# Sorted one-hot gathers in a graph transformer: twenty ranges of sixteen slots instead of twenty-two, with a pair's one-hots laid out by node block

## The chip, the cores and the metric

The kernel runs on one core of a Trainium2 chip. The metric is the device time of one execution in microseconds (us). TensorE does the matrix products, VectorE and ScalarE the elementwise work, GpSimd issues the indirect DMAs (gathers), and SyncE issues most of the other transfers. In the profile they are PE (PEld is its weight load), DVE, ACT, POOL and SP.

## The reference

Three layers of a graph transformer over 6250 nodes with 64 features and 206250 edges, sorted by destination:

```python
q, k, v, e = x @ Wq + bq, x @ Wk + bk, x @ Wv + bv, edge_attr @ We
alpha = sum(q[dst] * (k[src] + e), -1) / 8
p = exp(alpha - segment_max(alpha, dst)[dst])
w = p / segment_sum(p, dst)[dst]
x = relu(segment_sum((v[src] + e) * w, dst) + x @ Ws + bs)   # then a layer norm, in the first two layers
```

A log-softmax, a residual with the input and a last layer norm follow. What matters here is `x[src]`: for every edge, the 64 features of its source node.

## The kernel before

**Tiling.** Edges come in 403 chunks of 512 (four tiles of 128 rows). Four chunks make a unit; there are 100 whole units and a short rest in each layer. Nodes lie in 49 blocks of 128. Attention for a unit is: product with the queries (`scores`, L1648), maximum (L1655), exponential (L1662), transposed weights (`weights`, L1674, copied by L1677), weighted sums (`sums`, L1687, copied out by L1695).

**Two ways to fetch a source row.** One is a gather: an indirect DMA on POOL for 128 rows (`take`, L594). The other needs no DMA. The edges of a chunk are sorted once, in the first layer, so that the first `SLOTS = WINDOWS * SL` = 22 * 16 = 352 of its 512 places are *ranges*: range w holds 16 edges whose source lies in the four node blocks 2w to 2w+3. For such a range the rows come from a product of a one-hot matrix (which of the 128 nodes of a block does this edge want?) with the block's features, which lie in SBUF. Neighbouring ranges 2q and 2q+1 make a *pair*: range 2q takes blocks 4q to 4q+3, range 2q+1 takes blocks 4q+2 to 4q+5, so blocks 4q+2 and 4q+3 are in both.

**A job** is one pair for 16 chunks (`TURN` = 4 units), in class `Picker`. `load` (L1289) brings the pair's 512 keys (16 chunks, two ranges, 16 edges; place within the range's four blocks) to all partitions in one transfer of 128 rows of 1 KB. `aim` makes the one-hots: four DVE instructions of 128x512 (L1313), one for each of the four blocks of a range, both ranges at once. `bank` multiplies: for each of the two ranges, four products of 256 columns that add up in PSUM (L1352), 8 in all, and one ACT copy into `kept` (L1360). A pair's results serve four units, so with 11 pairs in layers 1 and 2 the units of a round of four have 3, 3, 3 and 2 jobs. In layer 0, `PAIRS[0]` = 6 pairs are used: 192 of a chunk's places, and only from unit 8 on.

**From `kept` to the unit.** `naturals` transposes and adds the two halves of the rows (L1387 in layers 1 and 2, L1376 in layer 0) and DVE copies them into the unit's `feat` (L1392, L1394). In layers 1 and 2 places 0 to 351 come that way: tiles 0 and 1 whole, and `PART` = 96 rows of tile 2. The other `REST` = 32 rows of tile 2, of four chunks, share one gather into the tile `few`, from which four ACT copies of 32 rows (`settle`, L611) take them to their places. Tile 3 is gathered for each chunk. So a unit has five gathers there. A gather waits for a copy of its indices into a `gate` by ACT (L631): that is how its place in time is set (`drip`, `free` and `release`; two units ahead of the unit that uses it).

**The first layer** also sorts: `ranking` seats the edges in ranges, one step for each of `WINDOWS + 1` = 23 kinds (L927, L931, L934, L938, L939), four rankings in all. `Move` reorders a unit's edges by products with 0/1 matrices of `REACH[t]` columns (L1052, L1063, L1077): for tile t of the unsorted edges, the sorted places up to which they can go. `Move.index` (L1108) derives the remaining source indices and writes the keys to DRAM (`keyS`, L1138) in pieces of 64 bytes. If the edges of some chunk do not fit the ranges and reaches, a flag is raised and a second, general program computes everything again after this one.

**Order.** The order is written out by hand. In the loop of layers 1 and 2 PE's order for a unit is: scores, naturals of the next unit, one `bank`, transposes of this unit's rows (L1635), weights, the remaining jobs that are due, sums. DVE's is: maximum, two copies of naturals, one-hots, copy of the weights, further one-hots. Two jobs' one-hots are ready ahead there, in two sets of four tiles; one in layer 0.

Of the kernel before, what the change touches and what calls it, by code (L numbers as in the profile page):

```python
# [36 lines left out]
WINDOWS = 22  # L37
# [14 lines left out]
REACH = (392, 416, 456, CH)  # L52
# [383 lines left out]
def main_path(  # L436
# [91 lines left out]
    def ps(tag):  # L528
        return psum.tile([P, 512], F32, tag=tag, name=f"ps_{tag}", bufs={"a": 2, "x": 2}.get(tag, 1))
# [3 lines left out]
    assert 2 * (WINDOWS - 1) + BW < NB <= 2 * BINS and NT % TURN == 0 and U0 % TURN == 0 and REST * LB == P  # L533
# [12 lines left out]
    keyS = dram.tile([KEYED, NT // TURN + 1, TURN, LB, 2 * SL], FP16, name="keyS")  # L546
# [9 lines left out]
    def fetch(layer, k):  # L556
# [15 lines left out]
        if layer and placed(layer, k):  # L572
            spares[layer, k] = later.tile([P, D], F32, name="few", bufs=FB + 1)

    def rows_wanted(layer, k):
# [6 lines left out]
        return [(None, 0)] + [(c, T - 1) for c in range(m)]  # L582

    def indices(layer, k, c, t):
# [3 lines left out]
        if c is None:  # L588
            return src_b, k * LB * T + (2 * LB - 1 if layer else LB + 1 + t // 2)
        return src_b, k * LB * T + t * LB + c  # L590

    def take(layer, k, c, t, index):

        nc.gpsimd.indirect_dma_start(  # L594
            out=loaded[layer, k][:, c, t, 0] if c is not None else spares[layer, k] if layer else loaded[0, k][:, t, 1, 0],
# [11 lines left out]
    def settle(layer, k):  # L607

        if layer and placed(layer, k):
            for c in range(LB):  # L610
                nc.scalar.copy(  # L611
                    loaded[layer, k][PART:, c, 2, 0], spares[layer, k][c * REST : (c + 1) * REST, :]
                )
# [257 lines left out]
    }  # L871
    stamps = [const.tile([P, LB * T, W], BF16, name=f"stamp{i}") for i in range(2)]
# [137 lines left out]
    class Move:  # L1010
# [97 lines left out]
        def index(self):  # L1108
# [3 lines left out]
            pi = pa[:, : 3 + 2 * LB]  # L1112
            pk = pa[:LB, W : W + KEYED * 2 * SL]
            nc.tensor.matmul(pk, keyc, self.to[:, : KEYED * 2 * SL], start=True, stop=True)
            for t in range(2, T):
                at = 3 + (t - 2) * LB
# [6 lines left out]
            for c in range(LB):  # L1123
                nc.tensor.matmul(
                    pi[c * REST : (c + 1) * REST, 2:3], self.to[:, SLOTS : 3 * P], pickc[:, c : c + 1], start=True, stop=True
                )
            nc.vector.tensor_scalar(
                src_b[:, k * LB * T + LB + 1 : (k + 1) * LB * T], pi, float(N - 1), None, ALU.min
# [133 lines left out]
    class Picker:  # L1262
# [14 lines left out]
        def load(self):  # L1277

            while self.loads and len(self.keys) < (7 if self.layer else 3):
# [3 lines left out]
                shape = [P, TURN * LB * 2 * SL]  # L1283
                if self.layer:
                    key = later.tile(shape, FP16, name="key", bufs=7)
                else:
                    key = picks.tile(shape, FP16, name="key", bufs=3)
                a, b = self.span(job)
# [749 lines left out]
```

## Time and profile before

| | |
|---|---|
| median of 3 runs | 4548.02 us (4546.31 to 4551.62) |
| profiled execution: time, span | 4547.86 us, 4546.1 us |
| busy share of the span: PE, PEld, DVE, ACT, POOL | 82%, 58%, 68%, 54%, 56% |
| mean granted TensorE clock | 0.895 |
| layer 0, steady part 300 to 2100 us: busy PE, DVE, ACT, POOL | 1503, 1216, 882, 1088 us of 1800 |
| layer 1, steady part 2420 to 3220 us: the same | 701, 602, 501, 469 us of 800 |
| layer 2, steady part 3560 to 4400 us: the same | 717, 634, 549, 480 us of 840 |

The span runs from the first to the last instruction of the profiled execution; 1.8 us of its time lie outside. Busy time of an engine is the union of its instructions. A matmul's duration includes the time in which its result still travels through the array, so consecutive ones overlap: what one costs PE is the distance between the starts of neighbours, which the timeline gives (a merged row of n instructions, and the start of the next row). A wait that is ascribed to an engine may have ended with another event at the same time. "remote" is an event whose origin the profile does not show.

### The profile page before, as it was taken

How to read it: one execution, taken by the hardware profiler on the slowest of the kernel's cores; microseconds unless marked ns; L12 is line 12 of the kernel's file. 1: busy time of each engine (PE TensorE's matmuls, PEld its weight loads, DVE VectorE, ACT ScalarE, POOL GpSimd, SP SyncE). 2: the span in 40 equal slices, each digit the busy share in tenths (PEclk: the TensorE clock that was granted, in tenths of full speed). 3: DMA queues.
4: the chain of work that ended last, by engine and by line, in shares of the span. 5: the costliest groups of instructions: out<-in, count | busy, mean ns of one | idle time of the engine just before them, and what ended most of it. 6: DMA issues, size and time to landing. Idle time of an engine off the chain costs nothing.

```text
span 4546.1 us, 106920 instructions
## 1 busy us (share of the span) xinstructions
PE 3750.4 (82%) x35698; PEld 2635.5 (58%) x35698; DVE 3110.5 (68%) x8905; ACT 2434.5 (54%) x6979; POOL 2547.7 (56%) x2094
## 2 busy tenths in 40 slices
PE   5778888888888888888789888888878888888885
PEld 2445555555555555555477666666747666666664
DVE  5566676776766766666477777777746777777784
ACT  2334544544545444544456666666645666666674
POOL 5545566666665665655265655565526655565653
PEclk9788998988989899998789999999878988899997
DMA  5446666667666677776467767777646776777774
GB/s 114 113 125 174 172 177 182 169 177 184 173 172 184 166 188 192 189 185 178 136 154 183 191 168 191 187 178 183 172 112 142 182 175 170 181 182 184 176 186 97
DMA packets 827547, 766.85 MB, mean 169 GB/s; under 512 B 395281, under 2 KB 624935, under 8 KB 826990
## 3 DMA queue, kind: packets, MB, share of 16 engines
q1 hardware_dynamic: 666370, 565.02, 49.8%
q0 software_dynamic: 66688, 68.42, 8.2%
q10 hardware_dynamic: 93932, 126.48, 7.9%
q8 instruction: 288, 4.72, 0.4%
q14 instruction: 269, 2.20, 0.2%
HBM read 599.30 MB, written 160.27 MB: 167 GB/s over the span
## 4 chain that ended last, share of the span: by engine, by line


## 5 line engine op out<-in xcount | busy, mean ns | idle before, releaser
L594 POOL DMA_INDIRECT feat<-in_x,gate x1044 | 1278.7, 1225 | 896.3 <-ACT gate L631 622.0
L1313 DVE TENSOR_SCALAR hot<-key,rank 128x512 fp32r<-128x512 f16 (+2 forms) x2832 | 1165.5, 474 | 144.4 <-DMA key<-keyS 34.6
L594 POOL DMA_INDIRECT feat<-x,gate x816 | 946.3, 1160 | 533.7 <-ACT gate L631 225.3
L1638 ACT COPY featT<-ps_a 64x512 f32<-64x512 f32 x1176 | 682.8, 581 | 86.3 <-remote 21.8
L1352 PE MATMUL ps_x<-hot,halves 128*128 128x256 f32 (+2 forms) x4368 | 684.1, 306 | 19.9 <-ACT kept L1360 9.0
L1352 PEld LDWEIGHTS ps_x<-hot,halves 128*128 128x128 f32 x4368 | 598.0, 202 | 31.8 <-ACT kept L1360 19.1
L1063 PE MATMUL ps_x<-hit,rest 128*64 128x512 bf16 (+3 forms) x3200 | 501.1, 391 | 11.0 <-issue 10.7
L1687 PE MATMUL ps_g<-feat,probT 128*32 128x128 f32 x9672 | 403.2, 295 | 117.7 <-issue 53.0
L594 POOL DMA_INDIRECT few<-x,gate x198 | 283.8, 1433 | 366.1 <-ACT gate L631 138.5
L1655 DVE TENSOR_REDUCE most<-ps_s 128x1 f32<-128x512 f32 x297 | 204.1, 687 | 391.3 <-PE ps_s L1648 156.6
L1052 DVE TENSOR_SCALAR hit<-ruler,pos 128x512 bf16<-128x512 f16 (+3 forms) x1600 | 421.6, 334 | 13.3 <-PE ps_m L1077 12.4
L1360 ACT CAST kept<-ps_x 128x512 fp32r<-128x512 f32 (+2 forms) x546 | 307.3, 582 | 218.1 <-PE ps_x L1352 137.0
L1648 PE MATMUL ps_s<-featT,q 128*32 128x512 f32 x2376 | 405.6, 640 | 11.2 <-issue 7.2
L1687 PEld LDWEIGHTS ps_g<-feat,probT 128*32 128x32 f32 x9672 | 287.1, 117 | 197.4 <-issue 104.5
L1635 PE MATMUL ps_a<-ident,feat 128*128 128x128 f32 x2348 | 353.1, 288 | 41.8 <-ACT gate L631 11.1
L1063 PE MATMUL ps_x<-hit,raw 128*64 128x512 bf16 (+3 forms) x1600 | 332.9, 404 | 8.0 <-issue 7.8
L631 ACT COPY gate<-src_b 128x1 int32<-128x1 int32 x1946 | 325.8, 191 | 20.7 <-ACT eN L1103 15.6
L1635 PEld LDWEIGHTS ps_a<-ident,feat 128*128 128x128 f32 x2348 | 288.6, 149 | 63.8 <-issue 23.2
L1387 PEld LDWEIGHTS ps_m<-twice,kept 128*128 128x128 f32 x1600 | 213.2, 206 | 186.9 <-issue 186.6
L1662 ACT ACTIVATE prob<-ps_s,part 128x512 f32<-128x512 f32 x297 | 204.3, 688 | 185.2 <-issue 33.2
L1063 PEld LDWEIGHTS <-rest 128*64 128x64 bf16 x3200 | 206.5, 123 | 162.3 <-issue 80.1
L1695 ACT COPY part<-ps_g 128x128 f32<-128x128 f32 (+1 forms) x309 | 82.6, 267 | 394.1 <-remote 124.9
(253 smaller groups left out, 5587.3 us busy)
## 6 DMA issues: line engine op xcount, KB each, us to landing
feat<-eaP SPq DMA_DIRECT2D x292, 512.0 KB
featT<-eaS SPq DMA_DIRECT2D x292, 512.0 KB
key<-keyS SPq DMA_DIRECT2D x668, 128.0 KB
raw<-in_ea SPq DMA_DIRECT2D x200, 256.0 KB
eaS<-eT ACTq DMA_DIRECT2D x200, 256.0 KB
eaP<-eN ACTq DMA_DIRECT2D x200, 256.0 KB
to<-toS SPq DMA_DIRECT2D x292, 128.0 KB
part<-part SPq DMA_DIRECT2D x600, 32.5 KB
```

Of the source, the lines that this page charges most:

```text
L594: nc.gpsimd.indirect_dma_start(out=loaded[layer, k][:, c, t, 0] if c is not None else spares[layer, k] if layer else loaded[0, k][:, t, 1, 0],
L631: copy(gate, index[:, i : i + 1])
L1052: nc.vector.tensor_scalar(hit, ruler[:, : REACH[t]], self.pos[:, at : at + 1], None, ALU.is_equal)
L1063: nc.tensor.matmul(self.px[i][j * D : (j + 1) * D, : REACH[t]], self.part(i, part)[:, (j * T + t) * D : (j * T + t + 1) * D], self.hits[t, ...
L1313: nc.vector.tensor_scalar(hot[:, a:b].rearrange("p k w e -> p (k w e)"), self.keys[job][:, a * 2 * SL : b * 2 * SL], rank[:, h : h + 1], None,
L1352: nc.tensor.matmul(px[:, w, a:b], halves[block >= EARLY][:, block - EARLY * (block >= EARLY)].rearrange("p h d -> p (h d)"), made[h][:, a: ...
L1360: nc.scalar.copy(kept[t][:, a:b, at : at + 2 * SL].rearrange("p k (w e) -> p w k e", w=2), px[:, :, a:b])
L1387: nc.tensor.matmul(pn[:, t - ts[0], c], kept[t][:, k % TURN * LB + c], twice, start=True, stop=True)
L1635: nc.tensor.transpose(pt[:, j - js[0], t // 2], rows[:, t * D : (t + 2) * D], ident)
L1638: nc.scalar.copy(featT[:, :, :, h, :], pt[h * D : (h + 1) * D])
L1648: nc.tensor.matmul(self.p_s[rows], self.q[:, j * STRIDE : j * STRIDE + W], self.featT[:, j, :], start=False, stop=True)
L1687: nc.tensor.matmul(p_g[rows, :].rearrange("n (h d) -> n h d", h=2), self.probT[:, t, rows], batch[:, c + j, t], start=(t == 0), stop=(t == ...
```

## The change

There are 20 ranges instead of 22 (`SLOTS` = 320), and the reaches go with it (376, 408, 464, 512 for 392, 416, 456, 512). Layers 1 and 2 use 10 pairs instead of 11, so a round of four units has 3, 3, 2 and 2 jobs. `PART` and `REST` are 64 and 64: the rest of tile 2 takes two gathers for a unit instead of one, and two ACT copies of 64 rows by 128 columns instead of four of 32 by 64.

The one-hots of a pair lie in one tile of eight pieces of 256 columns: block 4q, block 4q+1, block 4q+2 for both ranges, block 4q+3 for both ranges, block 4q+4, block 4q+5. Each of the four DVE instructions now writes two pieces that are not neighbours. A block that is in both ranges is multiplied once, with 512 columns; the four others with 256: 6 products for 8. The keys lie range by range, so a load brings two rows of 512 bytes to each partition, and the keys are written in pieces of 32 bytes. The two sets of one-hots are fixed tiles that are written again and again.

```diff
-WINDOWS = 22
+WINDOWS = 20
-REACH = (392, 416, 456, CH)
+REACH = (376, 408, 464, CH)
...
-        return [(None, 0)] + [(c, T - 1) for c in range(m)]
+        return [(None, c) for c in range(0, m, 2)] + [(c, T - 1) for c in range(m)]
...
-            for c in range(LB):
-                nc.scalar.copy(
-                    loaded[layer, k][PART:, c, 2, 0], spares[layer, k][c * REST : (c + 1) * REST, :]
-                )
+            for i in range(2):
+                nc.scalar.copy(loaded[layer, k][PART:, i::2, 2, 0], spares[layer, k][i * REST : (i + 1) * REST])
...
-                    nc.scalar.dma_start(keyS[those, job, r].rearrange("q c e -> c q e"), key[:, those])
+                    nc.scalar.dma_start(
+                        keyS[those, :, job, r].rearrange("q w c e -> c (q w) e"),
+                        key[:, those].rearrange("c q (w e) -> c (q w) e", w=2),
+                    )
...
-            made = []
-            for h in range(BW):
-                hot = pool.tile([P, TURN * LB, 2, SL], F32R, name="hot", bufs=BW)
+            made = hots[self.aimed % len(hots)]
+            for h, at in enumerate((slice(0, 4, 3), slice(1, 6, 4), slice(2, 7, 4), slice(4, 8, 3))):
                 nc.vector.tensor_scalar(
-                    hot[:, a:b].rearrange("p k w e -> p (k w e)"),
-                    self.keys[job][:, a * 2 * SL : b * 2 * SL],
+                    made[:, at, a * SL : b * SL],
+                    self.keys[job][:, :, a * SL : b * SL],
                     rank[:, h : h + 1],
                     None,
                     ALU.is_equal,
                 )
...
-            for w in range(2):
-                for h in range(BW):
-                    block = 2 * (2 * q + w) + h
-                    assert halved[block] == self.layer
-                    nc.tensor.matmul(
-                        px[:, w, a:b],
-                        halves[block >= EARLY][:, block - EARLY * (block >= EARLY)].rearrange("p h d -> p (h d)"),
-                        made[h][:, a:b, w],
-                        start=(h == 0),
-                        stop=(h == BW - 1),
-                    )
+            x = slice(a * SL, b * SL)
+            there = [px[:, :, x]] * 2 + [px[:, 0, x]] * 2 + [px[:, 1, x]] * 2
+            these = [made[:, 2:4, x], made[:, 4:6, x], made[:, 0, x], made[:, 1, x], made[:, 6, x], made[:, 7, x]]
+            for i, h in enumerate((2, 3, 0, 1, 4, 5)):
+                block = 4 * q + h
+                nc.tensor.matmul(
+                    there[i],
+                    halves[block >= EARLY][:, block - EARLY * (block >= EARLY)].rearrange("p h d -> p (h d)"),
+                    these[i],
+                    start=(i == 0),
+                    stop=(i == 5),
+                )
```

Two places in the order of the instructions, each before and then after. The first is PE in the steady part of layer 1, from the naturals of one unit to the sums; `ps_x` is a job's result, `prob` the weights.

```order
L1387 MATMUL ps_m<-twice,kept_32446 128x64 x4
L1387 MATMUL ps_g<-twice,kept_32447 96x64 x4
L1352 MATMUL ps_x<-hot,halves 128x256 x8
L1635 MATMUL ps_a<-ident,feat 128x128 x8
L1674 MATMUL ps_p<-ident,prob 128x128 x4
L1352 MATMUL ps_x<-hot,halves 128x256 x8
L1352 MATMUL ps_x<-hot,halves_32445 128x256 x8
L1687 MATMUL ps_g<-feat,probT 32x128 x16
```

```order
L1388 MATMUL ps_m<-twice,kept_31500 128x64 x4
L1388 MATMUL ps_g<-twice,kept_31501 64x64 x4
L1352 MATMUL ps_x<-hot,halves 128x512 x2
L1352 MATMUL ps_x<-hot,halves 128x256 x4
L1636 MATMUL ps_a<-ident,feat 128x128 x8
L1675 MATMUL ps_p<-ident,prob 128x128 x4
L1352 MATMUL ps_x<-hots_31499,halves 128x512 x2
L1352 MATMUL ps_x<-hots_31499,halves 128x256 x4
L1352 MATMUL ps_x<-hot,halves_31498 128x512 x2
L1352 MATMUL ps_x<-hot,halves_31498 128x256 x4
L1688 MATMUL ps_g<-feat,probT 32x128 x16
```

Nothing has changed its place: each job is six products instead of eight, and the naturals of tile 2 have 64 rows. The second place is ACT in layer 1, from one unit's `settle` to the next; `gate` releases a gather, `few` holds the rests of tile 2.

```order
L611 COPY feat<-few 32x64 x4
L1662 ACTIVATE prob,part<-ps_s,part 128x512
L631 COPY gate<-src_b 128x1
L1360 CAST kept_254<-ps_x 128x2x16x16
L1638 COPY featT<-ps_a 64x4x128
L631 COPY gate<-src_b 128x1
L1638 COPY featT<-ps_a 64x4x128 x2
L631 COPY gate<-src_b 128x1
L1638 COPY featT<-ps_a 64x4x128
L1360 CAST kept_32446<-ps_x 128x2x16x16
L1360 CAST kept_32447<-ps_x 128x2x16x16
```

```order
L611 COPY feat<-few 64x2x64 x2
L1663 ACTIVATE prob,part<-ps_s,part 128x512
L629 COPY gate<-src_b 128x1 x2
L1360 CAST kept_254<-ps_x 128x2x16x16
L1639 COPY featT<-ps_a 64x4x128 x2
L629 COPY gate<-src_b 128x1
L1639 COPY featT<-ps_a 64x4x128 x2
L629 COPY gate<-src_b 128x1
L1360 CAST kept_31500<-ps_x 128x2x16x16
L1360 CAST kept_31501<-ps_x 128x2x16x16
```

Both gathers of `few` are released together, right behind the exponential; the gathers of tile 3 follow at later points than before in the transposes' copies.

More of the change, by code (lines that the diff above doesn't have):

```diff
@@ L572, in fetch @@
         if layer and placed(layer, k):
-            spares[layer, k] = later.tile([P, D], F32, name="few", bufs=FB + 1)
+            spares[layer, k] = later.tile([P, LB // 2, D], F32, name="few", bufs=FB + 1)
     def rows_wanted(layer, k):
@@ L588, in indices @@
         if c is None:
-            return src_b, k * LB * T + (2 * LB - 1 if layer else LB + 1 + t // 2)
+            return src_b, k * LB * T + LB + t // 2 + (LB // 2 if layer else 0)
         return src_b, k * LB * T + t * LB + c
@@ L871, in main_path @@
     }
+    hots = [picks.tile([P, 2 * BW, TURN * LB * SL], F32R, name="hot", bufs=1)]
     stamps = [const.tile([P, LB * T, W], BF16, name=f"stamp{i}") for i in range(2)]
@@ L1111, in index @@
             pa = ps("a")
[L1112 removed]
+            pi = pa[:, : 3 * LB]
             pk = pa[:LB, W : W + KEYED * 2 * SL]
@@ L1319, in aim @@
                 )
-                made.append(hot)
             self.hots[job] = made
```

33 lines of the change are left out of this document (17 added, 16 removed).

## The prediction

> **What bounds the kernel now.** I read the busy shares first, then the busy times by stage, since half of the change touches layers 1 and 2 only.
>
> ```profile
> PE 3750.4 (82%) x35698; PEld 2635.5 (58%) x35698; DVE 3110.5 (68%) x8905; ACT 2434.5 (54%) x6979; POOL 2547.7 (56%) x2094
> ...
> 300.00:2100.00 1800.00, 1503.10 (x14672) 928.65 (x14668) 1215.60 (x3857) 881.61 (x2529) 1087.90 (x873) 0.90 0.67 178
> ...
> 2420.00:3220.00 800.00, 701.47 (x6978) 547.92 (x6968) 601.81 (x1502) 500.71 (x1458) 469.34 (x375) 0.94 0.73 182
> ```
>
> The columns of the last two rows are the stretch, its length, and PE, PEld, DVE, ACT and POOL busy, then granted clock, DMA share and GB/s. PE is busy 83% of layer 0 and 88% of layer 1, DVE 68% and 75%. No engine is full, but in layer 1 two come near it together. Next the groups of instructions between 2400 and 3200 us, to count work by unit.
>
> ```profile
> L594 POOL DMA_INDIRECT feat<-x,gate x299 | 355.6, 1189 | 187.5 <-ACT gate L631 81.6 <-issue 54.3 <-ACT feat L611 46.4
> L1313 DVE TENSOR_SCALAR hot<-key,rank 128x512 fp32r<-128x512 f16 x818 | 343.4, 484 | 28.2 <-PE ps_x L1352 13.8 <-remote 6.9 <-PE ps_p L1674 3.9
> L1352 PE MATMUL ps_x<-hot,halves 128*128 128x256 f32 x1640 | 254.6, 303 | 11.2 <-ACT kept L1360 5.3 <-DVE hot L1313 4.8 <-issue 1.0
> ...
> L594 POOL DMA_INDIRECT few<-x,gate x75 | 114.4, 1526 | 141.4 <-ACT gate L631 50.3 <-DVE feat L1394 32.2 <-PE ps_x L1352 22.9
> ...
> L1674 PE MATMUL ps_p<-ident,prob 128*128 128x128 f32 x296 | 46.7, 281 | 17.2 <-ACT prob L1662 13.8 <-issue 3.3
> ```
>
> L1674 runs four times a unit, so 74 units took 800 us: 10.8 us each. 1640 products are 205 jobs, 2.77 a unit. What a job costs PE is in the timeline of two undisturbed units (start, length):
>
> ```profile
> 2718.64 0.60 PE L1674 MATMUL ps_p<-ident,prob 128*128 128x128 f32 x4
> 2719.00 2.20 PE L1352 MATMUL ps_x<-hot,halves 128*128 128x256 f32 x16
> 2721.13 1.08 PE L1687 MATMUL ps_g<-feat,probT 128*32 128x128 f32 x32
> ...
> 2723.91 1.08 PE L1387 MATMUL ps_m<-twice,kept 128*128 128x64 f32 x8
> 2724.82 0.51 PE L1387 MATMUL ps_g<-twice,kept 128*96 128x64 f32 x4
> 2725.16 1.22 PE L1352 MATMUL ps_x<-hot,halves 128*128 128x256 f32 x8
> 2726.22 1.04 PE L1635 MATMUL ps_a<-ident,feat 128*128 128x128 f32 x8
> 2727.09 0.60 PE L1674 MATMUL ps_p<-ident,prob 128*128 128x128 f32 x4
> 2727.45 1.23 PE L1352 MATMUL ps_x<-hot,halves 128*128 128x256 f32 x8
> 2728.77 1.08 PE L1687 MATMUL ps_g<-feat,probT 128*32 128x128 f32 x32
> ...
> 2730.84 0.40 PE L1646 MATMUL ps_s<-to,codeT 128*32 128x512 bf16 x4
> ```
>
> No row shows a wait: from weights to weights PE ran through, 8.45 us. Eight products take 1.06 us from start to next start (2725.16 to 2726.22), 0.133 each. DVE in the same unit:
>
> ```profile
> 2726.45 1.67 DVE L1313 TENSOR_SCALAR hot<-key,rank 128x512 fp32r<-128x512 f16 x4
> 2728.04 0.68 DVE L1677 COPY probT<-ps_p 128x512 f32<-128x512 f32 x1
> 2728.64 1.66 DVE L1313 TENSOR_SCALAR hot<-key,rank 128x512 fp32r<-128x512 f16 x4
> ```
>
> A job's one-hots take 1.6 to 1.67 us of DVE, more than its products take of PE, and the sums at 2728.77 start when the copy of the weights ends (28.04 + 0.68). So in layers 1 and 2 the unit is paced by PE and DVE in turns, and a job taken away relieves both.
>
> **The change part by part, layers 1 and 2.** *Fewer jobs.* Ten pairs for eleven: 0.25 jobs fewer a unit. PE 0.25 x 1.06 = 0.27 us, DVE 0.25 x 1.66 = 0.42 us.
>
> *Six products for eight.* The columns are the same, 2048. Two pairs of 256 become two of 512. The trace has no such product of 512 columns. Were it still paced by its weight load it would take 0.133 (64 columns take nearly that: 2723.91 to 2724.82 is 0.114 for each of eight), and 0.266 if a column cost the same at any length. The step from 64 to 256 columns is only 0.019, so something other than columns paces the short ones, but 256 is where columns begin to show. I take 0.24, near the upper end: 2 x (0.266 - 0.24) = 0.05 us a job, 0.13 a unit; bounds 0 and 0.67. The Trainium skill ("TensorE: Matmul & The Clock Gate", Back-to-back issue gap) gives columns / 2.4 + 2.5 ns, an estimate of 109 ns for 256 and 216 for 512: by that the merging is worth 4 ns a job and speaks against this half of the change. The trace's 133 ns for 256 disagrees with its 109.
>
> *Fixed tiles.* DVE's first one-hot instruction writes the pieces that the first and third of six products read, and has to wait for the third of the job two before; it waited for the fifth of eight. The first product now needs three of the four instructions instead of one. Both cost nothing while a job's one-hots are ready two jobs ahead; without that lead the second would add two instructions, 0.83 us, to a job's start.
>
> *Naturals.* Four products with 96 weights' columns take 0.34 (2724.82 to 2725.16), 0.085 each, against 0.114 with 128. With 64 I extend that line: 0.057, so 0.11 us a unit less; 0 at worst. PE saves 0.27 + 0.13 + 0.11 = 0.51 us a unit.
>
> *ACT*, in the same unit:
>
> ```profile
> 2724.32 1.04 ACT L611 COPY feat<-few 32x64 f32<-32x64 f32 x4
> ...
> 2729.51 0.59 ACT L1360 CAST kept<-ps_x 128x512 fp32r<-128x512 f32 x1
> 2729.99 0.19 ACT L631 COPY gate<-src_b 128x1 int32<-128x1 int32 x1
> 2730.08 0.27 ACT L1695 COPY part<-ps_g 128x128 f32<-128x128 f32 x1
> ```
>
> It loses a quarter of a job's cast (0.25 x 0.48, from 2729.51 to 2729.99, = 0.12) and of settle about 0.50: four copies in 1.04, two of 128 columns at 0.27 by the L1695 row. It gains a gate, 0.19. About 0.43 us less a unit, on the way to the exponential that PE waits for.
>
> *One gather more.* POOL's rows:
>
> ```profile
> 2728.55 2.58 POOL L594 DMA_INDIRECT feat<-x,gate  x1 [0.30 <-ACT featT L1638]
> 2731.43 0.95 POOL L594 DMA_INDIRECT feat<-x,gate  x1 [0.30 <-issue]
> 2732.68 0.95 POOL L594 DMA_INDIRECT feat<-x,gate  x1 [0.30 <-issue]
> ```
>
> A gather is 0.95 at best, 0.30 apart; the mean is (355.6 + 114.4) / 374 = 1.26, so 1.56 us of POOL each. Five a unit are 7.8 us, six are 9.3. POOL is not touched on average at 10.4 us a unit, but units like the one above (8.45) are shorter than six gathers. They are released two units ahead of use, which covers short runs of such units. Without that cover, and if a third of the 200 units were that short (8.0 after the savings), each of these would wait 1.3 us: 90 us. I take 15. The 2.58 us lie where DVE writes one-hots (from 2728.64). The Trainium skill ("Advanced Engine Details and Errata", VectorE Performance Modes) says that DVE's two-port mode and GpSimd block each other; this row agrees, and fewer one-hots would then shorten the gathers a little.
>
> *Sum for a unit.* PE -0.51, DVE -0.42, ACT -0.43. As 12% of PE's time is waiting, on DVE and ACT, which also shrink, I let 0.45 us pass into the unit's length. 800 settle copies, four a unit, make 200 units:
>
> ```profile
> L611 ACT COPY feat<-few 32x64 f32<-32x64 f32 x800 | 193.2, 241 | 18.9
> L1352 PE MATMUL ps_g<-hot,halves 128*128 128x256 f32 (+3 forms) x1136 | 201.2, 319 | 35.7 <-ACT kept L1360 21.8 <-issue 7.7 <-DVE hot L1313 2.9
> L927 PE MATMUL ps_a<-past,kinds 128*96 128x512 bf16 (+3 forms) x368 | 85.7, 366 | 63.3 <-ACT featT L1638 37.5 <-DVE kinds L919 9.3 <-issue 6.9
> L1063 PE MATMUL ps_x<-hit,rest 128*64 128x512 bf16 (+3 forms) x3200 | 501.1, 391 | 11.0 <-issue 10.7
> ```
>
> 200 x 0.45 = 90 us, less 15 for POOL: 75.
>
> **Layer 0.** 1136 products are 142 jobs, as many as after: 142 x 0.05 = 7 us of PE. Ranking: 368 products are 92 steps, four rankings of 23; 21 each leaves 84. A step costs (85.7 + 63.3) / 92 = 1.6 us with its waits: 8 x 1.6 = 13. The reaches add up to 1760 columns for 1776, 0.9% of the rows at L1063 and its like: 4 us. Of these 24 us I take half, 12, since PE idles 16% of this stage.
>
> **The keys' transfers.** A load brings 256 rows of 512 bytes where it brought 128 of 1 KB, and the stores to DRAM have twice as many pieces.
>
> ```profile
> SPq L1289 <- DMA keyS<-key: 423.2, 69, 12.2
> ...
> q1 hardware_dynamic: 666370, 565.02, 49.8%
> ```
>
> The queue's packets take 0.498 x 16 x 4546 / 666370 = 0.054 us of one DMA engine each. The one-hots' rows give 708 loads before, 656 after: 168 thousand packets for 91, at most 260 us spread over 16 engines that are 67 to 73% busy; smaller packets should cost less each. The stores hold SP up in layer 0 already, 423 us in 69 waits with the loads for DVE and PE queued behind them. I cost both at nothing, since keys are fetched seven jobs ahead (three in layer 0); without that cover, 0.3 us more at each of the 69 waits is 20 us.
>
> **Sum.** 4547.86 - 75 - 12 = 4461, and the median before, 4548.02, differs from the profiled time by nothing that counts. I round up to **4464**, as a unit with two jobs already ends on the weights' copy and not on PE.
>
> **Rivals.**
>
> *POOL sets the pace.* Six gathers at 1.56 become the unit's length wherever it would be shorter than 9.3 us. For it: 88% of POOL's time by then, and single gathers of 2.58. Against: in the window POOL waits for ACT's gates (81.6 and 50.3 us), not they for it. Price: the 90 us above instead of 15, so about 4538; slower than before only if a gather's 1.56 rises to 1.8 (six are then 10.8, the present unit).
>
> *The one-hots get slower* (the other side). They are now written into two pieces 3 to 4 KB apart in one instruction; at present 512 elements take 0.415 us (1.66 / 4), while DVE's copy of 512 from PSUM takes 0.60 (2728.04 to 2728.64). If the new form fell to that, 10 instructions a unit cost 1.9 us more, 1.4 net of the 0.45, DVE becomes the bound, and 200 x 1.4 is +290 us: 4840. It decides from 0.46 us an instruction, where the gain is gone. Against: pieces are still 256 elements in a row. The page cited last ties the two-port rate to an even outermost count, which the two pieces have; no row shows that form.
>
> *The edges do not fit* twenty ranges, the flag is raised, and the general program runs as well: more than doubled time. Counted from the reference's indices, at most 42, 75 and 118 edges are left over after the first, second and third tile of any chunk, where 56, 88 and 144 fit, so this is all but excluded.
>
> **How the numbers follow.** Forecast, both engines relieved: 0.72, 4400 to 4510. POOL's pace: 0.17, of which a third no better than before. Slower one-hots 0.05, gathers past 1.8 us 0.05, not fitting 0.01. The range reaches from the upper ends of PE's terms held by DVE's (about 0.65 us a unit and all 24 of layer 0: 4394) to POOL eating everything: 4395 to 4550. A measurement of this kernel tells apart about 0.2%, 9 us: faster 0.82, same 0.07, slower 0.11.
>
> **What would show it.** Right: L1352 with two starts about 0.24 and four about 0.133 apart; about 2.5 jobs a unit; units near 10.3 us in layer 1; L1313's mean unchanged near 480 ns; POOL near 70% busy in layer 1. Wrong: PE or ACT waiting for gathers of `feat` or `few` with POOL back to back (rival 1); L1313 above 530 ns (rival 2); layer 0 shorter by far more or less than 12 us.

## The result and the profile after

The changed kernel took 4811.6 us (median of 4 runs, 4805.7 to 4813.4), the kernel before 4547.2 beside it (4531.2 to 4551.6): 1.060 of it, 95% interval 1.056 to 1.064. Forecast were 4464 us, and 4395 to 4550. The change made the kernel 6% slower.

Two lines of the changed kernel's page, its engines and its largest DMA queue:

```profile
PE 3748.5 (78%) x33938; PEld 2525.6 (53%) x33938; DVE 3016.0 (63%) x8663; ACT 2345.8 (49%) x6715; POOL 2625.0 (55%) x2294
...
q1 hardware_dynamic: 742850, 558.46, 46.9%
```

Work went away as it should: PE has 1760 matmuls fewer, DVE and ACT are busy for 95 and 89 us less. All shares of the span fell. Only POOL is busy for longer, 77 us with 200 gathers more. So no other engine has more to do, and all wait more. Where, a count of units says: a unit has four transposes of its weights, and the windows of that line alone count them. Columns: window, its length, PE busy and count, PEld busy and count, granted clock, DMA share, GB/s. The kernel before, line 1674, in layers 0, 1 and 2:

```profile
400.00:1600.00 1200.00, 38.53 (x232) 24.58 (x232) 0.90 0.67 177
2400.00:3200.00 800.00, 46.67 (x296) 34.47 (x296) 0.93 0.74 182
3600.00:4400.00 800.00, 48.88 (x300) 35.03 (x300) 0.92 0.73 180
```

The changed kernel, line 1675, in the same windows:

```profile
400.00:1600.00 1200.00, 38.90 (x220) 24.78 (x220) 0.88 0.64 168
2400.00:3200.00 800.00, 46.07 (x276) 34.76 (x276) 0.88 0.68 166
3600.00:4400.00 800.00, 46.81 (x268) 34.51 (x268) 0.87 0.68 164
```

58, 74 and 75 units became 55, 69 and 67. A unit of layer 1 grew from 10.8 to 11.6 us where 10.3 was forecast, and one of layer 0 from 20.7 to 21.8 (1200 / 55). Both kinds of layer lost, so two causes are possible, and TensorE's granted clock fell in all three. The groups of the changed kernel from 2400 to 3200 us:

```profile
L594 POOL DMA_INDIRECT feat<-x,gate x279 | 302.9, 1086 | 172.0 <-ACT gate L629 103.9 <-issue 59.9 <-ACT feat L611 3.9
L594 POOL DMA_INDIRECT few<-x,gate x138 | 190.0, 1377 | 137.7 <-ACT gate L629 105.6 <-issue 17.3 <-DVE hot L1312 4.7
...
L1312 DVE TENSOR_SCALAR hots<-key,rank 128x512 fp32r<-128x512 f16 x344 | 145.8, 482 | 16.2 <-remote 8.7 <-PE ps_x L1352 5.6 <-PE ps_p L1675 1.0
L1312 DVE TENSOR_SCALAR hot<-key,rank 128x512 fp32r<-128x512 f16 x344 | 145.6, 481 | 10.7 <-issue 4.4 <-PE ps_x L1352 3.0 <-remote 2.8
L1352 PE MATMUL ps_x<-hots,halves 128*128 128x512 f32 (+1 forms) x516 | 112.3, 358 | 5.3 <-issue 5.3
L1352 PE MATMUL ps_x<-hot,halves 128*128 128x512 f32 (+1 forms) x516 | 104.8, 340 | 6.6 <-ACT kept L1360 3.5 <-issue 2.0 <-DVE hot L1312 1.1
```

All that the forecast said of the work is there: 1032 products are 172 jobs on 69 units, 2.5 each; the one-hots take 481 and 482 ns; POOL waits for ACT's gates and is not behind. Six products take PE 1.02 us to the next start (2609.72 to 2610.74), where eight took 1.06:

```profile
2609.72 1.19 PE L1352 MATMUL ps_x<-hot,halves 128*128 128x512 f32 x6
2610.74 1.04 PE L1636 MATMUL ps_a<-ident,feat 128*128 128x128 f32 x8
```

Within a job the starts are 0.316, 0.233 and then 0.118 us apart (medians of 426 jobs of the trace at full clock). None of this says why a unit is longer.

### The profile page after: what moved, and what is told of

The parts are those of the page before. It is cut to its first block, busy times and chain, and to the rows that moved or that the text cites. A ratio compares the mean times of both kernels' runs of the same rounds, so it can differ in the third digit from the quotient of the medians.

```text
span 4803.8 us, 102550 instructions
## 1 busy us (share of the span) xinstructions
PE 3748.5 (78%) x33938; PEld 2525.6 (53%) x33938; DVE 3016.0 (63%) x8663; ACT 2345.8 (49%) x6715; POOL 2625.0 (55%) x2294
## 4 chain that ended last, share of the span: by engine, by line
## 5 line engine op out<-in xcount | busy, mean ns | idle before, releaser
L594 POOL DMA_INDIRECT feat<-in_x,gate x1044 | 1182.9, 1133 | 1085.2 <-ACT gate L629 753.1
L594 POOL DMA_INDIRECT feat<-x,gate x816 | 874.4, 1072 | 496.9 <-ACT gate L629 292.3
L594 POOL DMA_INDIRECT few<-x,gate x396 | 525.8, 1328 | 402.0 <-ACT gate L629 316.7
L1312 DVE TENSOR_SCALAR hot<-key,rank 128x512 fp32r<-128x512 f16 (+3 forms) x1600 | 665.2, 473 | 82.1 <-issue 28.7
L1688 PE MATMUL ps_g<-feat,probT 128*32 128x128 f32 x9672 | 426.7, 314 | 226.0 <-DVE probT L1678 122.1
L1312 DVE TENSOR_SCALAR hots<-key,rank 128x512 fp32r<-128x512 f16 (+1 forms) x1024 | 426.6, 475 | 39.9 <-remote 16.4
L629 ACT COPY gate<-src_b 128x1 int32<-128x1 int32 x2144 | 349.6, 190 | 97.1 <-ACT eT L1090 40.9
L1360 ACT CAST kept<-ps_x 128x512 fp32r<-128x512 f32 (+1 forms) x494 | 280.1, 581 | 232.8 <-remote 120.3
L1360 ACT CAST kept<-ps_g 128x512 fp32r<-128x512 f32 (+2 forms) x142 | 81.4, 573 | 518.9 <-PE ps_m L1076 156.1
L1352 PE MATMUL ps_x<-hots,halves 128*128 128x512 f32 (+2 forms) x1476 | 324.3, 361 | 12.9 <-DVE hots L1312 6.6
```

The source lines that it names most:

```text
L594: nc.gpsimd.indirect_dma_start(out=loaded[layer, k][:, c, t, 0] if c is not None else spares[layer, k][:, t // 2] if layer else loaded[0, ...
L629: copy(gate, index[:, i : i + 1])
L1312: nc.vector.tensor_scalar(made[:, at, a * SL : b * SL], self.keys[job][:, :, a * SL : b * SL], rank[:, h : h + 1], None, ALU.is_equal,)
L1352: nc.tensor.matmul(there[i], halves[block >= EARLY][:, block - EARLY * (block >= EARLY)].rearrange("p h d -> p (h d)"), these[i], start=(i ...
L1360: nc.scalar.copy(kept[t][:, a:b, at : at + 2 * SL].rearrange("p k (w e) -> p w k e", w=2), px[:, :, x].rearrange("p w (k e) -> p w k e", e ...
L1688: nc.tensor.matmul(p_g[rows, :].rearrange("n (h d) -> n h d", h=2), self.probT[:, t, rows], batch[:, c + j, t], start=(t == 0), stop=(t == ...
```

## The experiments

The kernel before takes 4507 to 4565 us on some chips (the result above is from such a one) and 3835 to 3840 on three others. Each chip was met on one occasion only, so whether the difference belongs to the chip or to the occasion is not shown. Every ratio is to the kernel before on the same chip; "the 4500 chips" and "the 3840 chips" name the two kinds.

| run | what it is | before, us | ratio (95%) |
|---|---|---|---|
| e1 | new layout, 22 ranges | 3838 | 1.003 (1.001 to 1.005) |
| e2 | 20 ranges, old layout | 3838 | 1.015 (1.011 to 1.018) |
| e3 | change, eight products | 3838 | 1.017 (1.013 to 1.022) |
| e4 | change, old keys | 3838 | 1.014 (1.011 to 1.018) |
| a5 | change | 4507 | 1.062 (1.058 to 1.067) |
| e6 | before, second gather | 4507 | 1.058 (1.052 to 1.065) |
| e7 | change, 4 steps in each ranking | 4507 | 1.040 (1.036 to 1.044) |
| f8 | change, 2 steps once | 3835 | 1.004 (1.001 to 1.006) |
| f9 | f8 without second gather | 3835 | 0.990 (0.987 to 0.993) |
| f10 | before, second gate only | 3835 | 1.002 (1.000 to 1.004) |
| f11 | before, plain copy | 3835 | 1.003 (1.001 to 1.004) |
| g12 | as e6 | 4565 | 1.063 (1.054 to 1.073) |
| g13 | before, second gather of 16 rows | 4565 | 1.061 (1.053 to 1.070) |
| g14 | before, POOL work | 4565 | 1.023 (1.015 to 1.031) |
| g15 | as e1 | 4565 | 0.997 (0.993 to 1.000) |
| h16 | as f9 | 3840 | 0.990 (0.987 to 0.993) |
| h17 | as f11 | 3840 | 1.002 (1.000 to 1.004) |

b5, the kernel before by itself on the chip of a5, took 4507.6 us in one run; it gives the trace.

### The change in halves: e1 to e4

The first theory (G) is that the second gather costs; the rival (D) that the new layout does. e1 is the changed kernel with twenty-two ranges and one gather again:

```diff
-WINDOWS = 20
+WINDOWS = 22
...
-REACH = (376, 408, 464, CH)
+REACH = (392, 416, 456, CH)
...
-        return [(None, c) for c in range(0, m, 2)] + [(c, T - 1) for c in range(m)]
+        return [(None, 0)] + [(c, T - 1) for c in range(m)]
```

> The second half of the change alone: twenty-two ranges and one gather of leftovers as before, with the new layout (keys range by range, fixed one-hot tiles, six products for eight). Theory G (the second gather of leftovers is what costs: transposes wait for rows, TensorE idles, its clock falls): the layout alone brings the forecast's 0.13 us of 200 units and a little of layer 0, so 4500 to 4535 us. Theory D (the layout costs, through the key transfers in twice as many pieces or through the fixed tiles): at least the 89 us that layer 0 lost, where the number of gathers is unchanged, so 4640 to 4800 us.

e2 is the reverse, these lines on the kernel before, with its keys, pooled one-hots and eight products:

> The first half of the change alone: twenty ranges, reaches and two gathers of leftovers as in the changed kernel, with the old keys, the old pooled one-hots and eight products. Theory G: 4750 to 4850 us, layer 0 as fast as before and layers 1 and 2 slower by 85 us each. Theory D: 4490 to 4530 us, the forecast less the gain of the six products.

e3 undoes the merged product only (`px[:, w, x]` and the four node blocks of each range in turn), e4 the keys' layout only:

```diff
-keyS = dram.tile([KEYED, 2, NT // TURN + 1, TURN, LB, SL], FP16, name="keyS")
+keyS = dram.tile([KEYED, NT // TURN + 1, TURN, LB, 2 * SL], FP16, name="keyS")
...
-                    self.keys[job][:, :, a * SL : b * SL],
+                    self.keys[job][:, a * 2 * SL : b * 2 * SL].rearrange("p (k w e) -> p w k e", w=2, e=SL),
```

> The changed kernel with eight products of 256 columns, each range by itself, on the new layout; all else as in the change. If the product with 512 columns is itself what costs (a longer hold of TensorE or of a bank), the time falls back to 4500 to 4600 us. Theories G and D: within 40 us of the changed kernel's 4811 us; a quarter of the products more makes it 0 to 40 us slower if TensorE's work sets the pace, and if a colder clock is what costs, the added work may bring 0 to 60 us back.

> The changed kernel with the keys stored and loaded as before (128 pieces of 1 KB for a job, not 256 of 512 bytes), the one-hot instructions reading them in pieces of sixteen. Theory D through the key transfers: 4450 to 4600 us, with layer 0 back where it was. Theory G, or D through the fixed tiles: within 30 us of 4811 us, plus what the one-hot instructions lose by the pieces (none to 0.3 us each for 2624 of them).

The layout alone is at 1.003; every one of these with twenty ranges is at 1.014 to 1.017, whatever its products and keys are. Theory D is out (g15 below repeats e1 on a 4500 chip, at 0.997). But the size fits no theory: the chip was a 3840 one, and theory G's place is wrong too. e2 does 68 units of layer 0 from 400 to 1600 us, e1 71, while in layers 1 and 2 they are within two units of each other. What cost here lay in layer 0, where the number of gathers did not change.

### The two suspects on one chip: a5, b5, e6, e7

In layer 0 the ranges set the length of a ranking: it is a generator with two steps for a range, and the sorter runs the first ranking to its end before its first move. Two ranges fewer are four steps fewer, so the first move comes earlier, and from there on the sorter's steps, four to a unit, lie elsewhere in the unit. The two traces show it: in unit 76 of the kernel before (b5) the products of an edge tile with 512 columns (L1063) are PE's last in the unit, behind both banks; in a5 they stand ahead of the scores, two of the four steps earlier. That the place of these steps costs is theory R. e7 pads every ranking of the changed kernel:

```diff
+        for _ in range(4):
+            yield
         left = sorts.tile([P, CH], FP16, name="order", bufs=1)[:n]
```

> The changed kernel with four empty steps in every ranking, so that a ranking takes as many steps of the schedule as with twenty-two ranges, with the work of twenty. Theory R: layer 0 gets back 30 to 50 us, 0.997 to 1.005 of before. Theory G: as the changed kernel beside it, within 15 us.

e6 puts a second gather, with the same indices, into the kernel before:

```diff
-        return [(None, 0)] + [(c, T - 1) for c in range(m)]
+        return [(None, c) for c in range(0, m, 2)] + [(c, T - 1) for c in range(m)]
```

> The kernel before with the gather of leftovers issued twice in layers 1 and 2 (the second into a tile that nobody reads), everything else as before. Theory G (the second gather costs: POOL and the transfers' queues): 1.008 to 1.02 of before, with layer 0 unchanged and units of layers 1 and 2 longer by 0.15 to 0.4 us. Theory R (it is the shorter ranking of layer 0, which shifts the order of its work by one step of a unit): 0.998 to 1.004.

> The changed kernel itself beside the first four runs' kind of chip, where the kernel before took 3838 us and not 4547. If the two halves of the change act as they did apart (1.003 and 1.0145 of before), it stands at 1.010 to 1.020 of before; if the loss of 6% belongs to the change wherever it runs, at 1.050 to 1.065.

> The kernel before again, for its trace on this chip: 1.000 of before by any theory. Units of layer 1 at 9.0 us here as in the three kernels with twenty ranges would say that fewer jobs save nothing on this chip; at 9.3 to 9.5 us that they save what the forecast said.

The chip was a 4500 one, and both theories hold, each in its own layers, at prices far above those expected (1.008 to 1.02 for e6, 30 to 50 us for e7). Units of the kernel before (b5), line 1674:

```profile
400.00:1600.00 1200.00, 38.71 (x236) 24.70 (x236) 0.91 0.67 180
2400.00:3200.00 800.00, 47.16 (x296) 35.29 (x296) 0.91 0.73 180
3600.00:4400.00 800.00, 50.12 (x302) 35.63 (x300) 0.92 0.73 181
```

The same with the second gather (e6):

```profile
400.00:1600.00 1200.00, 39.16 (x236) 25.01 (x236) 0.90 0.68 180
2400.00:3200.00 800.00, 46.37 (x268) 35.13 (x268) 0.88 0.68 167
3600.00:4400.00 800.00, 46.72 (x272) 33.89 (x272) 0.90 0.67 166
```

Layer 0 does 59 units in both. In the other two windows 149.5 units become 135: 10.70 and 11.85 us, so one gather costs 1.15 us of a unit in these windows, 230 us over 200 units, and the whole kernel is 265 us longer (4771 - 4507). The changed kernel (a5) does 55, 70 and 68 units, e7 60, 69 and 70: the ranking's steps bring back layer 0 and nothing else, 107 us (4793 - 4685).

What the displaced sorter does is seen at ACT's cast of a job's bank in layer 0, L1360. Its group from 400 to 1600 us in the kernel before, the row of the first profile:

```profile
L1360 ACT CAST kept<-ps_g 128x512 fp32r<-128x512 f32 x88 | 51.6, 586 | 127.0 <-remote 53.3 <-PE ps_m L1101 21.5 <-PE ps_g L1352 12.3
```

In the changed kernel, and then in e7:

```profile
L1360 ACT CAST kept<-ps_g 128x512 fp32r<-128x512 f32 x83 | 48.6, 585 | 314.2 <-PE ps_m L1076 101.9 <-PE ps_a L1100 80.0 <-remote 47.6
```

```profile
L1362 ACT CAST kept<-ps_g 128x512 fp32r<-128x512 f32 x89 | 52.2, 586 | 119.8 <-remote 42.0 <-PE ps_a L1127 23.9 <-PE ps_m L1102 21.0
```

ACT stands at this cast for 314 us instead of 127, and behind it on ACT are the transposes' copies, the exponential and the gates. With the sorter back in its place it is 120. One such stand, in a unit of a5; first PE:

```profile
1858.63 1.22 PE L1352 MATMUL ps_g<-hot,halves 128*128 128x512 f32 x6 [0.20 <-issue]
1859.69 0.60 PE L1636 MATMUL ps_a<-ident,feat 128*128 128x128 f32 x4
1860.22 0.59 PE L1076 MATMUL ps_m<-hit,stamp 128*32 128x512 bf16 x8
1860.75 0.66 PE L1100 MATMUL ps_a<-ident,eT 128*128 128x128 f32 x4
1868.80 2.05 PE L1352 MATMUL ps_g<-hot,halves 128*128 128x512 f32 x6 [7.40 <-DVE hot L1312]
```

and ACT in the same stretch:

```profile
1859.06 0.39 ACT L614 COPY feat<-feat 64x64 f32<-64x64 f32 x2
1867.84 0.59 ACT L1360 CAST kept<-ps_g 128x512 fp32r<-128x512 f32 x1 [8.39 <-remote]
1868.32 0.58 ACT L1639 COPY featT<-ps_a 64x512 f32<-64x512 f32 x1
1868.80 0.19 ACT L629 COPY gate<-src_b 128x1 int32<-128x1 int32 x1
```

The six products end at 1859.85 (1858.63 and 1.22), and the cast that needs them starts at 1867.84; "remote" names no engine or transfer of the core as its releaser. The trace records one signal of PE between 1858.5 and 1867.0 and then fifteen within 1.2 us, so by the trace the products were done and their signal came 8 us late. (The record of signals has gaps, but the cast's start does not depend on it.) "Remote" stands in all three rows of L1360 above, so late signals are not new; that a wait for "remote" is a late signal each time is read from this one.

In the traces of the ten runs that met a 3840 chip no wait ends with "remote", and there the displaced steps are seen by themselves. L1360 from 400 to 1600 us in e4 (short rankings), and then in f8, a run below that puts the steps back:

```profile
L1360 ACT CAST kept<-ps_g 128x512 fp32r<-128x512 f32 x103 | 60.4, 587 | 166.4 <-PE ps_g L1352 152.4 <-ACT eN L1102 9.7 <-PE ps_m L1076 3.8
```

```profile
L1362 ACT CAST kept<-ps_g 128x512 fp32r<-128x512 f32 x107 | 62.7, 586 | 65.4 <-PE ps_g L1354 45.3 <-ACT eN L1102 12.2 <-DMA raw<-in_ea 4.6
```

Of 166 and 65 us, 152 and 45 are waits for the cast's own products. So with the steps displaced ACT comes to the cast before its products are done; that on a 4500 chip late signals then make more of these waits is how I read the 314 us, and no run takes that apart.

### Steps and gather apart: f8 to f11

f8 pads the sorter once, at its start, and leaves the rankings short; f9 leaves out the second gather besides, and half of its leftover rows are those of the first.

```diff
         for i, _ in enumerate(first_ranks):
             if i % 2:
                 yield
+        for _ in range(2):
+            yield
```

```diff
     def take(layer, k, c, t, index):
+        if layer and c is None and t:
+            return
```

> The changed kernel with two empty steps of the sorter, once, between the first ranking and the first move; the later rankings stay short. If what layer 0 lost is the place of the sorter's four steps in a unit (theory R'), these two steps alone bring it back, as the four in every ranking did: 1.035 to 1.045 of before on a chip where before takes 4500 us, 0.997 to 1.006 where it takes 3840. If it is the number of steps of every ranking: no more than 30 us gained, 1.055 and 1.013.

> The same kernel with the second gather of leftovers left out in layers 1 and 2 (its gate is still copied; half of the leftover rows are those of the first gather, so this part of the output is not the reference's). Theory G: the forecast's gain comes out, 0.975 to 0.99 of before where before takes 4500 us and 0.985 to 1.0 where it takes 3840. If other parts of the change cost layers 1 and 2 their pace: within 0.01 of the kernel with two steps.

f10 has the second gate without the gather on the kernel before, f11 a plain transfer in its place:

```diff
+        if layer and c is None and t:
+            nc.sync.dma_start(spares[layer, k][:, 1], xts[layer][:P, :])
+            return
```

> The kernel before with a second gate copied on ACT for every unit of layers 1 and 2, and no gather behind it. If ACT's 0.19 us is what a second gather costs: 1.008 to 1.02 of before or more; theory G (the gather on POOL or its transfer): 0.998 to 1.005.

> The kernel before with the gate copied and a plain transfer of 128 rows of 256 bytes, issued by SP, where the second gather stood. If the transfer's pieces on the transfer engines cost: the 1.058 of the second gather where before takes 4500 us. If it is POOL's gather instruction: 1.000 to 1.015.

This was a 3840 chip. Two empty steps, once, take twenty ranges from 1.014 to 1.004 (71 units in layer 0's window, as in e1): it is the displacement, not the rankings' length. Without the second gather the kernel is at 0.990: the gather costs 51 us here, 0.26 us of a unit. The gate alone, and the gate with a plain transfer, put the kernel before at 1.002 and 1.003, about a fifth of that price. Where the 0.26 us go is seen at the first transposes of a unit. PE's group from 2000 to 2700 us in f8:

```profile
L1638 PE MATMUL ps_a<-ident,feat 128*128 128x128 f32 x623 | 84.9, 274 | 21.6 <-DMA feat<-x,gate 21.4
```

and in f9:

```profile
L1640 PE MATMUL ps_a<-ident,feat 128*128 128x128 f32 x624 | 81.5, 274 | 3.4 <-DMA feat<-x,gate 3.4
```

18 us over 77 units are 0.23 us a unit of PE waiting for gathered rows. Not all of it is gained, as another wait grows: over layers 1 and 2 whole (from 1900 us) PE waits 85 us for gathered rows in f8 and 23 in f9, but 106 and 133 us for ACT's exponential. The balance is 36 of the 51 us. POOL in f8, same window:

```profile
L594 POOL DMA_INDIRECT feat<-x,gate x313 | 360.6, 1152 | 95.4 <-issue 55.5 <-ACT gate L629 13.4 <-ACT feat L611 6.1
L594 POOL DMA_INDIRECT few<-x,gate x156 | 182.8, 1172 | 64.8 <-ACT gate L629 27.6 <-issue 18.9 <-PE ps_x L1354 4.0
```

543 us of gathers and 0.3 us behind each of 469 are 684 of 700: POOL is full, at 700 / 77 = 9.1 us a unit. On these chips the first rival came true.

### What of a gather costs: g12 to g15

On a 4500 chip POOL is not full (417 gathers, 493 us and 0.3 behind each, 618 of 800 in the changed kernel), so 1.15 us need another reason. g12 repeats e6, g13 makes the second gather one of 16 rows, g14 puts two iotas on POOL in its place, g15 repeats e1.

```diff
+        if layer and c is None and t:
+            nc.gpsimd.indirect_dma_start(out=spares[layer, k][:16, 1], ...
+                in_offset=bass.IndirectOffsetOnAxis(ap=index[:16], axis=0))
+            return
```

```diff
+        if layer and c is None and t:
+            idle = later.tile([P, CH], FP16, name="idle", bufs=1)
+            for _ in range(2):
+                nc.gpsimd.iota(idle, pattern=[[1, CH]], ...)
+            return
```

> The second gather of leftovers on the kernel before, once more, as the measure for the two runs after it. Theory G: 1.05 to 1.065 of before where before takes 4500 us, 1.008 to 1.02 where it takes 3840 (there the kernel without the second gather was 0.0137 faster than with it).

> The kernel before with a second gather of 16 rows, not 128. If the rows are what costs (their descriptors and the transfers): an eighth to a quarter of what the second gather of 128 rows costs. If it is the instruction itself, its place in POOL's queue and its wait: half of it or more.

> The kernel before with two iotas on POOL (some 0.55 us each in the page of before) in place of the second gather, and no transfer. If the later gathers lose because POOL comes to them later: as much as the second gather. If it is what the gather sends out: within 0.004 of before.

> The new layout with twenty-two ranges once more. Theory G: 0.985 to 1.000 of before where before takes 4500 us (the fewer products are TensorE's, which is colder there), 1.000 to 1.005 where it takes 3840, as in its first run.

Sixteen rows cost what 128 do. POOL's time, its gate and the changed release points cost 0.023, about a third, which lies between the two outcomes expected. The other 0.04 come with the gather itself, whatever the number of its rows. The Trainium skill ("DMA: Bandwidth & Descriptors", Why a DMA increments its semaphore by 16 and not by 1) says that a transfer issued from GpSimd has 16 completions whatever its shape; 16 rows at the price of 128 agree with a price of completions, but no run shows it. POOL's rows in g13 from 2400 to 3200 us, the 128-row gather of leftovers and the one of 16:

```profile
L602 POOL DMA_INDIRECT few<-x,gate x66 | 84.7, 1283 | 153.3 <-ACT gate L639 144.9 <-issue 7.8 <-ACT feat L619 0.3
L595 POOL DMA_INDIRECT few<-x,gate x66 | 63.6, 964 | 20.1 <-issue 9.1 <-DVE hot L1321 6.1 <-DMA part<-part 1.5
```

POOL itself saves 0.32 us on the small one, and no unit is shorter for it (66 in the window, as in g12).

Where the 1.15 us go is seen at TensorE's clock and in its waits. Windows of five units running of e6 in layer 1, columns as on the page (the granted clock is the first number behind POOL's):

```profile
3005.30:3021.90 16.60, 13.08 (x99) 8.00 (x98) 10.44 (x27) 7.77 (x24) 9.99 (x10) 0.79 0.76 173
3021.90:3038.70 16.80, 13.52 (x102) 11.09 (x100) 10.29 (x32) 9.74 (x24) 7.67 (x8) 0.71 0.45 115
3038.70:3048.20 9.50, 9.40 (x94) 7.05 (x93) 8.40 (x22) 6.13 (x21) 5.13 (x6) 0.98 0.75 181
3048.20:3055.80 7.60, 7.59 (x91) 6.05 (x90) 5.11 (x12) 5.19 (x18) 6.38 (x5) 1.00 0.70 156
3055.80:3071.70 15.90, 10.85 (x96) 8.25 (x94) 9.18 (x22) 7.65 (x23) 8.24 (x9) 0.79 0.63 173
```

Two units at full clock take 7.6 and 9.5 us, three that met a lowered clock 16 to 17, with about the same instructions. Counted over 2400 to 3200 us: in b5 18 of 74 units have 2 us or more of lowered clock and take 15.0 us on average, in e6 24 of 67, at 15.7; units with under 0.5 us of it take 9.4 and 9.7. So (24/67) x 6.0 - (18/74) x 5.5 = 0.8 us of the difference are more units that meet the lowered clock, and 0.3 that the others are longer. That is not the clock's doing alone. The same stretch as a whole, b5 and then e6 (behind the length, PE, PEld, DVE, ACT and POOL busy):

```profile
2400.00:3200.00 800.00, 708.65 (x6925) 554.69 (x6926) 596.97 (x1496) 497.82 (x1447) 440.89 (x372) 0.91 0.73 180
```

```profile
2400.00:3200.00 800.00, 683.61 (x6295) 524.85 (x6293) 546.03 (x1355) 458.99 (x1377) 464.60 (x407) 0.88 0.68 167
```

In a unit PE is busy for 9.6 us in b5 and 10.2 in e6, and idle for 1.2 and 1.7: about 0.6 us are slower instructions and 0.5 are waits. The waits come first. PE in e6 just ahead of two falls of the clock, each with the lowered stretch behind it (PE busy, granted clock, DMA share, GB/s):

```profile
3008.33:3011.74 3.41, 1.89 (x21) 1.00 0.90 166
3011.74:3018.57 6.83, 4.83 (x15) 0.50 0.71 137
3025.40:3028.81 3.41, 0.13 (x5) 1.00 0.88 180
3028.81:3039.05 10.24, 10.24 (x50) 0.50 0.36 103
```

The clock falls 27 times between 2400 and 3200 us of e6. In the 3.41 us ahead of a fall PE was busy for 0.36 of the time (the median; 0.67 at most), in the other stretches of that length at full clock for 0.99. In b5 there are 17 falls, with 0.37 (0.50 at most) and 1.00. The lowered stretches last 3.4 us or a multiple of it, in this window of e6 up to 17 us. The Trainium skill ("TensorE: Matmul & The Clock Gate", Part 1) has the clock halve after an idle window of about 3.4 us and return after a busy one; the lengths agree. The windows ahead of a fall were not all idle, only less busy than the rest.

Those waits are hardly for gathered rows: PE's waits for these are 4.4 us of this window in e6. A part of them are late signals. ACT's waits for "remote" at a job's cast in the same window, in b5, e6, g13 and g14 (us in total, times, longest):

```profile
ACT kept L1360 <- remote: 11.4, 5, 4.3
ACT kept L1360 <- remote: 38.7, 16, 7.0
ACT kept L1368 <- remote: 47.6, 23, 6.6
ACT kept L1365 <- remote: 3.3, 1, 3.3
```

All engines' waits for "remote" together are 74 us in b5 and 79 in g15, 139, 159 and 124 in e6, g12 and g13, and 45 in g14. So a second gather, of 128 rows or of 16, goes with late signals, and POOL's work in its place does not. Why it does is not shown. On a 3840 chip a unit with a lowered clock loses little: 9.4 us against 8.8 in f8.

### Twice more: h16, h17

> The changed kernel with the two empty steps and without the second gather once more (its gate is copied; half of the leftover rows are those of the first gather, so this part of the output is not the reference's). Where before takes 4500 us: 0.975 to 0.99 if the forecast's other terms hold there, 0.995 to 1.02 if the slow chip loses something else with twenty ranges. Where it takes 3840: 0.990 again.

> The kernel before with the gate copied and a plain transfer of 128 rows of 256 bytes, issued by SP, where the second gather stood, once more. Where before takes 4500 us: 1.04 to 1.065 if any transfer more costs there (its completions), 1.00 to 1.02 if it is the gather instruction on POOL. Where it takes 3840: 1.003 again.

They met a 3840 chip again and repeat f9 and f11. Whether a plain transfer, or only POOL's gather, costs 6% on a 4500 chip stays open, and so does what holds the signals up there. A version with twenty ranges in which one gather brings all leftovers was not made: 64 leftover rows in each of four chunks are two times 128.

## Why the prediction was wrong, by its steps

On the chip of a5 the sum can be closed, if the two costs add up: +265 (second gather, e6) and +107 (sorter's place, e7) leave 286 - 372 = -86 us for all else, some 34 us either way by the intervals of e6 and e7. The forecast had -90 for the units' work and -12 for layer 0. There its savings were about right; of the two costs it had one at 15 us and the other not at all. On a 3840 chip the kernel without the two costs, except for the second gate (f9), is at 0.990: 38 us saved, less than half of the 102. So that the savings came out on one kind of chip is in part luck.

**The step that failed: one gather more at 15 us, at most 90.** It costs 265 and about 280 us on the 4500 chips (e6, g12) and 51 on a 3840 one (f8 to f9; h16 repeats f9's ratio). The price was made of POOL's time and of the cover of two units ahead. On the 3840 chips this was the right mechanism with too small a price: POOL was taken as busy for 9.3 of a 10.4 us unit, and the unit there is 9.1. On the 4500 chips it was the wrong mechanism: POOL had time, sixteen rows cost as much, PE hardly waited for gathered rows, and the loss is waits, in part for late signals, and the clock that falls behind them. What makes signals late when a gather is added stays open.

**The second that failed: the shorter ranking, part of a gain of 12 us in layer 0.** Only the rankings' work was counted. That the sorter's first move waits for their steps (two for each kind, not one) was not seen, though the code says it. It cost 107 us on the 4500 chip and 0.010 to 0.013 of the time, 40 to 50 us, on the 3840 chips (e2, e3 and e4 beside f8).

**Fewer jobs.** Right: 2.5 a unit. Beside the same second gather, 11.85 us (e6) became 11.59 (a5) and 11.51 (e7), 0.26 to 0.34 us of the 0.45 for PE, DVE and ACT together.

**Six products for eight.** Right in the piece: 1.02 us for a job where eight took 1.06, so 0.04 for the 0.05 forecast, though the starts are not 0.24 and 0.133 apart but 0.316, 0.233 and 0.118. (The 0.133 was a mean: of the eight, the first start is 0.202 ahead of the next and the others 0.122, medians of 508 jobs in the trace of before.) In time it is nearly nothing: the layout alone is 0.997 on one chip and 1.003 on another (forecast 0.993: 0.13 us of 200 units and 7 us), and e3, which has the eight, is no different from e2 and e4.

**Fixed one-hot tiles, key transfers.** At nothing, right: e3, e4 and e2 (new keys, old keys, neither) are 1.017, 1.014 and 1.015 with overlapping intervals. The queue's packets rose by 76 thousand and its share fell with the longer span.

**Rivals.** Slower one-hots: no, 481 ns. Edges that don't fit: no. POOL's pace: on one kind of chip, at a little over half of its price (51 of 90 us). Of the forecast's signs of being right, jobs and one-hots came as said in a kernel that was 6% slower, the pitch nearly, and POOL at 61% of layer 1 for near 70: they were signs of the work. The only one that spoke of time, units near 10.3 us, failed, and a sign of being wrong, layer 0's time, was seen.

## What to carry to other kernels

In a kernel whose engines all wait on one another, price an instruction that is added to every round by adding it to the kernel as it is and measuring that: its own duration says little, and one gather more cost 265 us here where 15 were forecast from its rows. Where a table of sizes also sets how many steps a generator has, a smaller size moves everything that is started by counting those steps; pad the steps first, and time the work afterwards. A share that falls on all engines at once is a count of waits, and the units that paid are found by their granted clock.

## What the runs showed of the hardware

- One kernel, the one before, takes 3835 to 3840 us on three chips and 4507 to 4565 on others. Instructions of DVE last as long (a one-hot 474 ns in b5, 472 in f10, the kernel before with a second gate); granted clock and waits differ: 0.96 (f10) and 0.90 or 0.91 (before, b5) in layer 0.
- On a 4500 chip a signal from PE came 8 us after the instruction had ended (1859.85 to 1867.84). Waits of that kind ("remote") stand in all ten traces from 4500 chips and in none of the ten from 3840 chips.
- A gather of 16 rows more costs this kernel as much as one of 128 more (1.061 and 1.063), and both bring more such waits (124 and 159 us of 800 for 79 in g15).
- TensorE's clock fell right after 3.41 us in which it was busy for 0.36 of the time (e6, median of 27), where 0.99 is usual.
